# Routing eight images' tokens in groups of one, two, three and two instead of four pairs, with the gate's top two by two maxima

## The chip, the cores and the metric

The kernel runs on one core of one Trainium2 chip. A core has five engines that run side by side, each on its own list of instructions: TensorE (PE; PEld is its loading of weights), VectorE (DVE), ScalarE (ACT), GpSimd (POOL) and SyncE (SP), which here issues the plain DMAs. They wait for each other by semaphores. The metric is the time of one execution on the device in microseconds, from the first to the last instruction with what little lies around it; lower is better.

## What is computed

The input is 8 images of 256 channels and 32 x 32 points, in float32. Two layers follow each other. Cut to what matters:

```python
# layer 0
x = x + vim_block(_ln_c(x))          # a selective scan over the 1024 points, 512 inner channels, 16 states
t = tokens(x)                        # 8 x 1024 tokens of 256
t = t + moe(_ln_t(t))
# moe: 8 experts, each 256 -> 512 -> 256 with gelu; every token takes its two best
probs = softmax(xf @ gate_w + gate_b)
top2_vals, top2_idx = top_k(probs, 2)          # ties: the lower index first
cw = zeros.at[arange(N)[:, None], top2_idx].add(top2_vals)
out = sum over e of cw[:, e] * (gelu(xf @ W1[e] + b1[e]) @ W2[e] + b2[e])
# layer 1
x = x + concat(x_id, conv3x3(x_hw), conv1x11(x_w), conv11x1(x_h), mamba(x_mb))(_ln_c(x))
t = t + mixture_of_depths(_ln_t(t))  # the 511 of 1024 tokens of an image with the largest weights
                                     # pass 256 -> 1024 -> 256, the others stay
```

The routing is independent for each token, so tokens may be gathered and sent to the experts in groups of any size.

## The kernel before

**Units, groups and pairs.** A unit is half an image (512 points). For each of the 16 units layer 0 prepares (`unit_prep`: norm, projections, short convolution, dt) and scans (`scan_unit`): four chunks of 128 channels by 16 states, each with an exponential on ScalarE (L826), a scan on VectorE (L829), a product with C (L834), and the sum over states as matmuls into PSUM (L845). The products with B come from GpSimd (L821), where some pairs of states are added too (L838; how many of the eight pairs of a unit is in `PAIRED`, one entry a unit and four more for the second layer). Rows of B and C come by DMA (`bc`, L880). `tokens` then projects back, writes the tokens to DRAM (`gx`) and makes the gate's logits.

A group is a pair of images, four units, 16 blocks of 128 tokens (NB = 16). When its last unit is done, these follow:

- `route` (L968 to L1101), on VectorE with little else: a softmax over 8 logits; `better` (L999), in eight parts, which compares every logit with every other (128 elements an instruction) and counts how many beat it; `masks` for the first and the second; `counts`, `sums`, `ends`, `ends2`, which give every choice a row in a list sorted by expert and padded to blocks of 256 rows; `pick`, the row's number and the weight for each of the two choices; and the weights turned for the experts' biases (`cwt`).
- `scatter`: each token's normed row is written twice into that list (`slots_x`, DRAM) by indirect DMAs from GpSimd's queue (L1113), 32 for a group.
- `experts`: a group of NB blocks has at most 2 x NB x 128 / 256 + 7 blocks of 256 rows, 23 here. Each reads its rows, one expert's weights (1 MB), turns the rows (L1187), and does two products (L1202 and L1224, gelu on ScalarE between, L1208). Its result leaves PSUM at L1252 and goes to `slots_y`. A block may not start before all row writes of its group have landed.
- `combine`: each token's two result rows come back by indirect DMAs (L1300), are weighted and added, for pairs 0 and 1 by matmuls (L1312 to L1315), for pairs 2 and 3 on VectorE; then layer 1 begins for the same pair: norm, the four convolution branches (`taps_of`, L1391), `mamba_in`, `mamba_scan` (the lines of the unit's scan again), `mamba_out`, `assemble`.
- `ranks` (comparisons of every token's weight with all others, L1601 and L1606), `feed_forward` (row writes, then four blocks of two halves on L1202 and L1224) and `finish`.

**What sets the order.** The whole program is a list of steps, each with an engine, an estimated duration, a priority and the buffers it reads and fills. A planner (`Flow.run`, in Python, before the launch) hands the steps to the engines one by one: of those whose inputs will be ready and whose buffers are free it takes the smallest priority, with some leave to fill gaps. Each engine then runs its steps in that written order, and SP its DMAs. Priorities are positions on one scale: unit i's scan stands at UNIT_AT[i] = 16 + 32 i and takes 32 positions, so the last ends at 544. `PLAN` holds for each pair the positions of its later stages, as (start, step) where there are several parts: `experts=(180, 8.0)` puts block b at 180 + 8 b. Where the planner sees PE idle for over 0.7 us it puts fillers, small matmuls of zeros (L560, L564).

**Buffers.** `logits` has two buffers of [128, 16, 8], `slots_x` two and `slots_y` two lists of 23 x 256 rows in DRAM, `xg` two tiles (a third and fourth once the units are done), `xz` one. The lists `slots_x` are cleared once at the start (`clear_slots`).

Of the kernel before, what the change touches and what calls it, by code (L numbers as in the profile page):

```python
# [47 lines left out]
NB = 16  # L48
NI = NB // 2
SB = 256  # L50

NX = 2 * NB * P // SB + E - 1
# [4 lines left out]
PAIRED = [4, 1, 0, 3, 0, 4, 7, 4, 4, 6, 8, 8, 5, 5, 5, 6, 8, 8, 6, 1]  # L57
# [5 lines left out]
    dict(put=3.51, experts=(180, 8.0), combine=(398, 2.34), taps=(451, 3.28), mamba=464, assemble=(496, 1.12), ranks=500, ffn=(524, 4.8), finish=(613, 2.76)),  # L63
    dict(put=4.68, experts=(357, 6.25), combine=(505, 1.88), taps=(585, 1.2), mamba=551, assemble=(563, 2.41), ranks=620, ffn=(745, 3.84), finish=(768, 4.5)),
    dict(put=5.28, experts=(465, 5), combine=(562, 2.94), taps=(679, 2.65), mamba=643, assemble=(689, 1.5), ranks=682, ffn=(788, 1.69), finish=(797, 4.62)),
    dict(put=2.65, experts=(603, 4), combine=(692, 0.33), taps=(755, 1.54), mamba=775, assemble=(776, 0.43), ranks=753, ffn=(812, 2.4), finish=(841, 3.07)),
# [254 lines left out]
def layers(g, ctx, x, a, out):  # L321
# [71 lines left out]
    first = g.t(w, [P, E, E], "first")  # L393
    nc.gpsimd.memset(first, 0.0)
    for e in range(1, E):
        nc.gpsimd.memset(first[:, e, :e], 1.0)

# [15 lines left out]

    carry = g.t(w, [P, E, NB], "carry")
    nc.gpsimd.memset(carry, 1.0)
    nc.gpsimd.memset(carry[:, :, 0:1], 0.0)

# [36 lines left out]
    groups = [{} for _ in range(B // 2)]  # L454
# [18 lines left out]
    def x_tile(i):  # L473
# [31 lines left out]
        "logits": tiles("logits", [P, NB, E], 2),  # L505
# [5 lines left out]
        "cwt": tiles("cwt", [P, P], 2),  # L511
        "xg": tiles("xg", [P, 2, C], 2, in_order=False),
        "slots_y": tiles("slots_y", [NX * SB, C], 2, where=g.dram),
# [393 lines left out]
    def tokens(i, prio):  # L907

        u = units[i]
        grp, q = groups[i // 4], i % 4  # L910
# [57 lines left out]
    def route(n, prio):  # L968

        grp = groups[n]  # L970
        wide = [P, NB, E]
        r, lg = buf("sq"), grp["logits"]
# [9 lines left out]

        def softmax():
            one = small([P, NB, 1], 0)
            nc.vector.tensor_reduce(one, lg.v, AX.X, ALU.max)
            nc.vector.tensor_tensor(lg.v, lg.v, one.to_broadcast(wide), ALU.subtract)

        def softmax2():
            tot = small([P, NB, 1], 0)
            nc.vector.tensor_reduce(tot, lg.v, AX.X, ALU.add)  # L990
            nc.vector.reciprocal(tot, tot)
            nc.vector.tensor_tensor(lg.v, lg.v, tot.to_broadcast(wide), ALU.mult)


        part_of = [P, NB // 8, E, E]

        def better(part):
            blks = slice(part * NB // 8, (part + 1) * NB // 8)
            gt, eq = small(part_of, 128), small(part_of, 256)  # L999
            mine = lg.v[:, blks].unsqueeze(3).to_broadcast(part_of)  # L1000
            other = lg.v[:, blks].unsqueeze(2).to_broadcast(part_of)
            nc.vector.tensor_tensor(gt, other, mine, ALU.is_gt)
            nc.vector.tensor_tensor(eq, other, mine, ALU.is_equal)
            nc.vector.tensor_tensor(eq, eq, first.unsqueeze(1).to_broadcast(part_of), ALU.mult)
            nc.vector.tensor_tensor(gt, gt, eq, ALU.add)
            nc.vector.tensor_reduce(small(wide, 0)[:, blks], gt, AX.X, ALU.add)

        def sels():
            return [small(wide, 384 + 128 * i) for i in range(3)]

        def masks():
            rank = small(wide, 0)
            sel, sel1, sel2 = sels()
            nc.vector.tensor_scalar(sel, rank, 1.5, None, ALU.is_lt)
            nc.vector.tensor_scalar(sel1, rank, 0.5, None, ALU.is_lt)
# [891 lines left out]
```

## Time and profile before

| | |
|---|---|
| time, median of 3 runs | 3679.84 us (3678.03 to 3680.75) |
| the profiled execution: its time / its span | 3683.03 / 3681.0 us |
| mean granted TensorE clock | 0.946 |
| instructions | 37,497 |
| moved by DMA | 676.61 MB, mean 184 GB/s |

Read by stage: up to about 800 us only units run; from then on the expert blocks of the first groups run beside the scans; pair 0's second layer begins near 1730 us; the last unit's scan ends near 2805 us; then come the last group's routing, its blocks, and the rest of the second layer for pairs 1, 2 and 3. An engine's busy share says little alone: matmuls overlap, so a busy PE isn't PE at its peak, and an engine may be idle where another holds it up.

### The profile page before, as it was taken

The page shows a single profiled execution, that of the slowest core. Times are in us where ns is not written, and L with a number is a line of the kernel's source. Part 1 is how long each engine was busy: PE and PEld are TensorE (multiplying, and loading weights), DVE is VectorE, ACT ScalarE, POOL GpSimd, SP SyncE. Part 2 cuts the span into 40 slices and gives each one's busy share as a digit, 9 for nine tenths or more (in the row PEclk, how much of TensorE's full clock was granted, in tenths as well). Part 3 has the DMA queues.
Part 4 walks back from the last instruction along what each step waited for, and adds up shares of the span by engine and source line. Part 5 has one row for each costly group of instructions (what it writes and reads, how often), then busy time and mean ns, then how long its engine had stood idle before and what let it go on. Part 6 is the DMA issues. An engine that isn't in the chain of part 4 may idle for free. (4 is left out here: it accounts for less than half of the span.)

```text
span 3681.0 us, 37497 instructions
## 1 busy us (share of the span) xinstructions
PE 3211.1 (87%) x10567; PEld 1807.2 (49%) x10567; DVE 2918.0 (79%) x4181; ACT 2188.2 (59%) x3985; POOL 2407.4 (65%) x1751
## 2 busy tenths in 40 slices
PE   8889888889889988978998898988888888899858
PEld 3334333334445444444554445555546565685536
DVE  4889889989778987986988789768698938965951
ACT  4555455467567656755875675655675546747533
POOL 3767567487867758986986887654786743716522
PEclk9999999999999999999999999999999988999989
DMA  6334333346445445644654557565657786877756
GB/s 231 132 132 138 110 125 129 107 161 209 159 133 172 167 134 174 203 155 147 211 178 164 179 178 240 190 197 161 195 180 261 234 258 206 307 230 244 265 168 190
DMA packets 276301, 676.61 MB, mean 184 GB/s; under 512 B 31015, under 2 KB 114861, under 8 KB 276094
## 3 DMA queue, kind: packets, MB, share of 16 engines
q1 hardware_dynamic: 257662, 623.87, 51.6%
q0 software_dynamic: 18432, 50.36, 4.2%
q8 instruction: 84, 1.38, 0.2%
q14 instruction: 123, 1.01, 0.1%
HBM read 572.92 MB, written 101.19 MB: 183 GB/s over the span
## 5 line engine op out<-in xcount | busy, mean ns | idle before, releaser
L821 POOL TENSOR_TENSOR dbu<-dtx,bc 128x1024 f32<-128x1024 f32 x551 | 1300.8, 2374 | 239.7 <-PE y L845 119.6
L845 PE MATMUL y<-dbu,ident 128*128 128x512 f32 x1616 | 837.4, 630 | 174.9 <-POOL dbu L838 129.5
L826 ACT ACTIVATE mm<-dt,neg_a 128x512 f32<-128x512 f32 x1152 | 767.7, 688 | 172.9 <-DVE dbu L834 150.6
L829 DVE TENSOR_TENSOR_SCAN mm<-mm,dbu 128x512 f32<-128x512 f32 x566 | 691.9, 1222 | 211.3 <-ACT mm L826 176.7
L834 DVE TENSOR_TENSOR dbu<-mm,bc 128x512 f32<-128x512 f32 x1104 | 763.3, 691 | 53.1 <-PE mm L1202 0.5
L829 DVE TENSOR_TENSOR_SCAN mm<-mm,state,dbu 128x512 f32<-128x512 f32 x560 | 717.6, 1281 | 40.0 <-ACT mm L826 25.4
L838 POOL TENSOR_TENSOR dbu<-dbu 128x512 f32<-128x512 f32 x318 | 412.0, 1296 | 294.6 <-DVE dbu L834 277.6
L845 PEld LDWEIGHTS y<-dbu,ident 128*128 128x128 f32 x1616 | 291.5, 195 | 537.8 <-issue 211.9
L833 ACT COPY state<-mm 128x1 f32<-128x1 f32 x576 | 91.8, 160 | 701.3 <-DVE dbu L834 660.6
L1224 PE MATMUL mm<-we,hid 128*128 128x256 f32 x1536 | 370.6, 394 | 34.3 <-ACT hid L1208 23.2
L1202 PE MATMUL mm<-xbt,we 128*128 128x256 f32 x1632 | 384.1, 386 | 17.9 <-ACT xbt L1190 10.3
L1202 PEld LDWEIGHTS mm<-xbt,we 128*128 128x128 f32 x1632 | 312.0, 193 | 106.1 <-issue 30.9
L1224 PEld LDWEIGHTS mm<-we,hid 128*128 128x128 f32 x1536 | 296.6, 197 | 116.0 <-ACT hid L1208 35.5
L756 PE MATMUL mm<-pre,w_tap 128*128 128x512 f32 (+3 forms) x512 | 245.2, 622 | 28.8 <-ACT pre L743 27.7
L1300 POOL DMA_INDIRECT ys<-slots_y,slot x128 | 126.9, 992 | 184.8 <-DMA xb<-slots_t 71.3
L560 PE MATMUL y<-still 128*128 128x512 bf16 x924 | 237.5, 392 | 0.0
L462 ACT ACT_TABLE_LOAD x166 | 213.0, 1283 | 3.0
L1208 ACT ACTIVATE hid<-mm,we 128x256 f32<-128x256 f32 x408 | 161.5, 475 | 33.9 <-PE mm L1202 25.1
L756 PEld LDWEIGHTS mm<-pre,w_tap 128*128 128x128 f32 x512 | 97.3, 197 | 167.2 <-issue 106.1
L1688 POOL DMA_INDIRECT ys<-y,slot_t x64 | 64.2, 1003 | 172.8 <-DVE xc L1698 81.0
L560 PEld LDWEIGHTS <-still 128*128 128x128 bf16 x924 | 92.6, 101 | 159.5 <-issue 93.0
L1113 POOL DMA_INDIRECT slots_x<-xg,slot x120 | 122.4, 1020 | 30.8 <-issue 19.7
(279 smaller groups left out, 4476.7 us busy)
## 6 DMA issues: line engine op xcount, KB each, us to landing
bc<-rows SPq DMA_DIRECT2D x610, 512.0 KB
we<-in_W SPq DMA_DIRECT2D x82, 514.0 KB
we<-in_W SPq DMA_DIRECT2D x77, 512.0 KB
xb<-slots_x SPq DMA_DIRECT2D x92, 256.0 KB
slots_y<-xo SPq DMA_DIRECT2D x92, 256.0 KB
xc<-x SPq DMA_DIRECT2D x64, 256.0 KB
we<-in_W12f SPq DMA_DIRECT2D x20, 514.0 KB
slots_x<-xg SPq DMA_DIRECT2D x10, 1024.0 KB
```

The costliest lines, as they stand in the source:

```text
L462: nc.scalar.preload_act_table_set(tables[name])
L560: nc.tensor.matmul(live[0].v[:, 0], still, wide, start=False, stop=False)
L756: nc.tensor.matmul(tc_.v[:, cut:], w_tap[:, c, j], pre.v[:, cut + j : j + N], start=j == 3, stop=j == 0)
L821: gpsimd(2.45, prio, lambda: nc.gpsimd.tensor_tensor(dbu.v, dtxs.v[:, n : n + 1].to_broadcast(wide2), bt.v, ALU.mult), [dtxs, bt], [dbu], ...
L826: step(ACT, 0.69, prio, lambda j=j, h=h: nc.scalar.activation(h.v, dts.v[:, n], AF.Exp, scale=scales(j)), [dts], [h], table="exp", scan=True)
L829: step(DVE, 1.25, prio, lambda j=j, h=h: nc.vector.tensor_tensor_scan(h.v, h.v, dbu.v[:, j], 0.0 if initial is None else initial[1](j), AL ...
L834: step(DVE, 0.68, prio, lambda j=j, h=h: nc.vector.tensor_tensor(dbu.v[:, j], h.v, ct.v[:, j], ALU.mult), [h, ct], [dbu], scan=True)
L838: gpsimd(1.3, prio + 2.3, lambda: nc.gpsimd.tensor_tensor(dbu.v[:, 0], dbu.v[:, 0], dbu.v[:, 1], ALU.add), [], [dbu])
L845: nc.tensor.matmul(y.v[:, n], g.ident, dbu.v[:, j], start=False, stop=stop and (paired or j == 1))
L1202: nc.tensor.matmul(tv[:, f], we[0].v[:, at : at + P], xbt.v[:, k], start=k == 0, stop=k == KC - 1)
L1208: nc.scalar.activation(hid.v[:, f], tv[:, f % 2], func, bias=we[0].v[:, at : at + 1])
L1224: nc.tensor.matmul(to, hid.v[:, f, h * P : (h + 1) * P], we[1].v[:, f * C : (f + 1) * C], start=extra is None and f == 0, stop=f == FC - 1,)
```

## The change

Five things are changed together.

1. **Groups.** `GROUPS = [1, 2, 3, 2]`: image 0 alone, images 1 and 2, images 3 to 5, images 6 and 7. A group is routed when its last image's units are done. Groups have 8, 16, 24 and 16 blocks of tokens and `blocks_of(nb)` = 15, 23, 31 and 23 blocks of rows. Tiles are sized for the largest (NB = 24).
2. **Pairs stay for layer 1.** `combine` and all that follows still goes by pairs of images; pair 0 takes results of groups 0 and 1, pair 1 of groups 1 and 2, pairs 2 and 3 of one group each. The load that opens a combination waits for the results of both groups.
3. **Gate by two maxima.** Instead of the comparisons and the masks, `choose` takes the maximum, marks where it is equal, weights the marks by 8 - e (`turn_of`) and takes their maximum, so that one is left, the lowest index; then the same with 2 taken off the chosen one.
4. **Buffers.** `logits` has one buffer instead of two, `slots_y` three instead of two, `cwt` room for a second turned part (the group of three has 192 columns); `xz` is gone and its tile is taken from `xg`; `first` and `carry` are gone, the latter is filled anew in each `sums`.
5. **Places.** `PLAN` and `PAIRED` have new numbers.

```diff
-NB = 16
-NI = NB // 2
+NI = 8
+GROUPS = [1, 2, 3, 2]
+NB = NI * max(GROUPS)
...
+def blocks_of(nb):
+    return 2 * nb * P // SB + E - 1
+NX = blocks_of(NB)
...
-PAIRED = [4, 1, 0, 3, 0, 4, 7, 4, 4, 6, 8, 8, 5, 5, 5, 6, 8, 8, 6, 1]
+PAIRED = [4, 1, 0, 3, 0, 4, 7, 4, 5, 7, 8, 8, 5, 3, 5, 6, 8, 5, 6, 0]
...
-    dict(put=3.51, experts=(180, 8.0), combine=(398, 2.34), taps=(451, 3.28), mamba=464, assemble=(496, 1.12), ranks=500, ffn=(524, 4.8), finish=(613, 2.76)),
-    dict(put=4.68, experts=(357, 6.25), combine=(505, 1.88), taps=(585, 1.2), mamba=551, assemble=(563, 2.41), ranks=620, ffn=(745, 3.84), finish=(768, 4.5)),
-    dict(put=5.28, experts=(465, 5), combine=(562, 2.94), taps=(679, 2.65), mamba=643, assemble=(689, 1.5), ranks=682, ffn=(788, 1.69), finish=(797, 4.62)),
-    dict(put=2.65, experts=(603, 4), combine=(692, 0.33), taps=(755, 1.54), mamba=775, assemble=(776, 0.43), ranks=753, ffn=(812, 2.4), finish=(841, 3.07)),
+    dict(put=1.76, experts=(110, 12.0), combine=(368, 2.34), taps=(474, 4.1), mamba=464, assemble=(501, 1.41), ranks=482, ffn=(514, 4.8), finish=(608, 2.76)),
+    dict(put=4.68, experts=(249, 7.0), combine=(535, 1.9), taps=(590, 0.72), mamba=595, assemble=(595, 2.0), ranks=668, ffn=(750, 3.84), finish=(776, 4.5)),
+    dict(put=5.28, experts=(411, 4.0), combine=(545, 2.9), taps=(679, 2.65), mamba=643, assemble=(679, 1.5), ranks=690, ffn=(808, 1.69), finish=(794, 4.62)),
+    dict(put=2.65, experts=(597, 4.0), combine=(612, 0.32), taps=(765, 1.54), mamba=715, assemble=(726, 0.69), ranks=753, ffn=(812, 2.4), finish=(853, 3.07)),
...
+    turn_of = g.t(w, [P, 1, E], "turn_of")
+    nc.vector.tensor_scalar(turn_of[:, 0], count[:, :E], -1.0, float(E), ALU.mult, ALU.add)
...
-        "logits": tiles("logits", [P, NB, E], 2),
+        "logits": tiles("logits", [P, NB, E], 1),
...
-        "cwt": tiles("cwt", [P, P], 2),
+        "cwt": tiles("cwt", [P, -(-NB // 16), P], 2),
...
-        "slots_y": tiles("slots_y", [NX * SB, C], 2, where=g.dram),
+        "slots_y": tiles("slots_y", [NX * SB, C], 3, where=g.dram),
...
-        def better(part):
-            blks = slice(part * NB // 8, (part + 1) * NB // 8)
-            gt, eq = small(part_of, 128), small(part_of, 256)
-            mine = lg.v[:, blks].unsqueeze(3).to_broadcast(part_of)
-            other = lg.v[:, blks].unsqueeze(2).to_broadcast(part_of)
-            nc.vector.tensor_tensor(gt, other, mine, ALU.is_gt)
-            nc.vector.tensor_tensor(eq, other, mine, ALU.is_equal)
-            nc.vector.tensor_tensor(eq, eq, first.unsqueeze(1).to_broadcast(part_of), ALU.mult)
-            nc.vector.tensor_tensor(gt, gt, eq, ALU.add)
-            nc.vector.tensor_reduce(small(wide, 0)[:, blks], gt, AX.X, ALU.add)
...
+        def choose(i):
+            left, one, same = small(wide, each), small([P, nb, 1], 5 * each), small(wide, 0)
+            sel, sel1, sel2 = sels()
+            if i:
+                nc.vector.scalar_tensor_tensor(left, sel1, -2.0, lgv(), ALU.mult, ALU.add)
+            val, to = (left, sel2) if i else (lgv(), sel1)
+            nc.vector.tensor_reduce(one, val, AX.X, ALU.max)
+            nc.vector.tensor_tensor(same, val, one.to_broadcast(wide), ALU.is_equal)
+            nc.vector.tensor_tensor(same, same, turn_of.to_broadcast(wide), ALU.mult)
+            nc.vector.tensor_reduce(one, same, AX.X, ALU.max)
+            nc.vector.tensor_tensor(to, same, one.to_broadcast(wide), ALU.is_equal)
+            if i:
+                nc.vector.tensor_tensor(sel, sel1, sel2, ALU.add)
...
+            carry = small([P, E, nb], 2 * each)
+            nc.vector.memset(carry, 1.0)
+            nc.vector.memset(carry[:, :, 0:1], 0.0)
...
-        for part in range(8):
-            step(DVE, 1.9, prio + 1 + 0.25 * part, lambda part=part: better(part), [lg], [r])
-        step(DVE, 0.6, prio + 3, masks, [], [r])
+        for i in range(2):
+            step(DVE, 1.4 + 0.5 * i, prio + 1 + i, lambda i=i: choose(i), [lg], [r])
...
-        for b in range(NX):
+        for b in range(blocks_of(grp["nb"])):
...
-        "xz": tiles("xz", [P, 2, 2 * P], 1),
...
+        both = [groups[group_of[2 * n + i]]["y"] for i in range(2)]
...
-                xc.v, grp["gx"].v[:, at : at + 2]), [grp["gx"], grp["y"]], [xc], claims=[at_a, at_b]).opens = line
+                xc.v, moe["gx"].v[:, at : at + 2]), [moe["gx"], *both], [xc], claims=[at_a, at_b]).opens = line
...
+            if i == 0:
+                xz = buf("xg")
...
-        if i % 4 == 3:
-            n = i // 4
+        b = i // 2
+        n = group_of[b]
+        if i % 2 and b == groups[n]["last"]:
             at = PLAN[n]
             route(n, end + 12)
             scatter(n, end + 16, at["put"])
             experts(n, *at["experts"])
-            combine(n, *at["combine"])
...
+            for n in range(groups[n]["first"] // 2, (b + 1) // 2):
+                at = PLAN[n]
+                combine(n, *at["combine"])
...
+                finish(n, *at["finish"])
```

## The prediction

> **What bounds the kernel now.** I read the page first (shares per engine), then the busy time by stage, then the groups of instructions by line, the waits, and last the stretch after the last scan in order of time. The stages are cut where the work changes: no expert block before 800 us, scans beside blocks to 2800, routing of the last group to 2980, its blocks to 3290, the last pair's second layer to 3535, and a closing chain. Columns: stretch, its length, busy us (instructions) of PE, PEld, DVE, ACT and POOL, granted clock, DMA share, GB/s.
>
> ```profile
> span 3681.0 us, 37497 instructions
> PE 3211.1 (87%) x10567; PEld 1807.2 (49%) x10567; DVE 2918.0 (79%) x4181; ACT 2188.2 (59%) x3985; POOL 2407.4 (65%) x1751
> ...
> 0.00:800.00 800.00, 693.52 (x1793) 295.44 (x1793) 665.64 (x836) 416.40 (x764) 500.56 (x331) 0.94 0.41 139
> 800.00:2000.00 1200.00, 1065.71 (x3352) 575.10 (x3352) 1007.70 (x1257) 781.11 (x1390) 941.62 (x643) 0.97 0.52 171
> 2000.00:2800.00 800.00, 706.48 (x2315) 409.21 (x2314) 663.70 (x886) 521.13 (x938) 563.13 (x396) 0.94 0.60 192
> 2800.00:2980.00 180.00, 149.40 (x628) 111.16 (x627) 134.69 (x196) 98.80 (x182) 102.74 (x103) 0.95 0.72 238
> 2980.00:3290.00 310.00, 273.21 (x1164) 201.20 (x1163) 226.87 (x537) 185.92 (x351) 133.44 (x115) 0.93 0.79 259
> 3290.00:3535.00 245.00, 223.67 (x890) 145.26 (x891) 182.68 (x355) 137.22 (x265) 122.03 (x110) 0.96 0.70 233
> 3535.00:3681.00 146.00, 99.07 (x432) 69.79 (x430) 36.71 (x118) 47.59 (x98) 43.92 (x55) 0.84 0.58 180
> ```
>
> To 2800 us VectorE is busy 83 to 84% of every stage and the others wait for it. The longest wait of all is ScalarE's for VectorE's product with C (L834). After 2800 TensorE is the fullest, at 83 to 91%, and at the very end nobody is: one chain runs.
>
> ```profile
> ACT state L833 <- DVE dbu L834: 660.6, 467, 8.0
> POOL dbu L838 <- DVE dbu L834: 277.6, 161, 10.0
> ```
>
> The gate is VectorE work. Its five instructions, 32 of each (eight parts in each of four groups): name, shapes, count, busy us, mean ns, idle before.
>
> ```profile
> L1002 DVE TENSOR_TENSOR sq<-logits 128x128 f32<-128x128 f32 x32 | 21.9, 683 | 0.7
> L1004 DVE TENSOR_TENSOR sq<-sq,first 128x128 f32<-128x128 f32 x32 | 19.5, 610 | 1.1
> L1003 DVE TENSOR_TENSOR sq<-logits 128x128 f32<-128x128 f32 x32 | 18.8, 587 | 0.0
> L1005 DVE TENSOR_TENSOR sq<-sq 128x128 f32<-128x128 f32 x32 | 12.5, 389 | 1.1
> L1006 DVE TENSOR_REDUCE sq<-sq 128x16 f32<-128x128 f32 x32 | 9.2, 286 | 1.1
> ```
>
> The last group's way from gate to experts, in order of time: the gate's first and last instruction on VectorE, the last of 32 row writes on POOL, the first block's transposes on PE (start, length).
>
> ```profile
> 2825.89 0.29 DVE L985 TENSOR_REDUCE sq<-logits 128x16 f32<-128x128 f32 x1 [1.48 <-POOL logits L962]
> 2899.17 0.28 DVE L1083 TENSOR_TENSOR sq<-sq,logits 128x128 f32<-128x128 f32 x1
> 2955.81 0.96 POOL L1113 DMA_INDIRECT slots_x<-xg,slot  x1 [0.19 <-issue]
> 2983.29 0.60 PE L1187 MATMUL mm<-ident,xb 128*128 128x128 f32 x4
> ```
>
> So 157 us pass, 73 of them in a gate whose own instructions fill some 38; the other 35 are pair 1's scans (L829) and taps (L1391).
>
> **The change, part by part.** The sum is made against the profiled execution, 3683.03 us (span 3681.0 and 2.0 around it), which is 3.2 above the median of 3679.84.
>
> *Gate.* Removed: 81.9 us of comparisons (the five rows) and the masks, four times three instructions of 226, 218 and 530 ns, 3.9 us. Added per group: 4 reductions (286 ns, the L1006 row) and 8 with two inputs (567 ns, the mean of the first four rows), 5.7 us; two small fills and one more sum, 0.9. Four groups: 26.4. Net -59 us of VectorE, 14.8 a group. Uncontended, at the medians of 292 ns of the same rows, 46.6 would go and 18 come: -30 with masks. If the new ones hardly wait and the old waits vanish, -69. I take 59: these are means over the places where the gate runs. [...] The trace's means decide.
>
> Three of the four gates lie before 2800, where VectorE is busy 0.85 of the time (2290 of 2700 us from 100 us on); what it saves there turns into time by about that share: 3 x 14.8 x 0.85 = **-38** (bounds 0 and -52). If VectorE were hidden there, the cover would be ScalarE's exponentials (688 ns each), and the term is 0.
>
> *Blocks.* Their number is unchanged: a group of n images has 8n + 7, so 15 + 23 + 31 + 23 = 92 against four times 23. PE's expert work stays. What moves is when they can run: the first 15 from position 110 instead of 23 from 180. Block evictions (L1252) by stage are now 0, 32, 30, 7 and 23 or 24; so 7 blocks of the first three groups run after 2800. At the tail's own pace (transposes 8.3 us apart between 3215 and 3256) these are 58 us of PE. Started some 250 us earlier, at the 2.7 blocks per 100 us of the stage from 800 on, 7 blocks are in front by 800 us, so the backlog goes. Against that pair 1's combination, now at 2553 to 2669, must wait for group 2 and falls near or behind 2800: 128 matmuls at 0.22 us (16 take 3.62) are 28 us. Net -30, times PE's share of 0.88 from 2980 to 3290: **-26**. Bounds: 0 (PE not the limit) and -58. [...]
>
> *Cost of an early block on the scans.* A block uses no VectorE; VectorE idles 11.5% from 100 to 800 without blocks and 16% from 800 to 2000 with 2.7 per 100 us, about 1.3 to 1.7 us a block, paid now wherever the block stands: **0**. If the earlier, denser scans suffer more: +20 (15 blocks), bound below -10.
>
> *Last gate.* Its own 15 us go, and pair 1's scans and taps move from positions 551 and 585 to 595 and 590, behind the gate at 556: up to 50 of its 73 us. Its row writes (32, one per 1.27 us, at least 41 us of the 53) now share POOL's queue with gathers of two combinations instead of one, placed at 535 and 545: 32 gathers at 1.0 us, of which I let 24 fall into it. **-26**, bounds -60 and +20. The blocks behind it wait for all the writes, and PE has little else then.
>
> *The tail's order.* Pair 3's combination 692 to 612, scan 775 to 715, assembly 776 to 726, its feed-forward unmoved at 812, its end 841 to 853; pair 2's feed-forward 788 to 808. PE does only fillers and closing transposes for 50 us from 3536, so a feed-forward left over for there would gain up to 50; queues crossed badly on SP or POOL lose as much. **0**, bounds -50 and +50. In the same way pairs 0's places (combination 398 to 368, taps 451 to 474, ranks 500 to 482) are 0 within ±15.
>
> *Small ones, together 0 within -10 and +25.* Clearing 31 instead of 23 blocks of two buffers is 16 transfers of 1 MB for 12, 4.2 MB, 18 us of DMA at the first 100 us' 231 GB/s, on SP's queue among the row loads for which POOL already waits 74 us before 800; the DMA share of 0.41 there hides it. The combination's turned tile now takes one of xg's buffers and can hold up a row write. The combination's load waits for both groups' results; behind it in SP's order stand later loads, whose users are later too. The paired additions stay 70 for the units and fall from 23 to 19 for the second layer: 8 fewer on POOL at 1.3 us, 16 more matmul instructions at 0.63. A second transpose and eviction in the group of three: 0.3 and 0.4.
>
> Sum: -38 - 26 - 26 = -90; 3683 - 90 = 3593, and 3590 against the median.
>
> **The rivals.**
> 1. *Pair 1 is pushed too far (slower).* Its combination needs the 31 blocks of group 2. From 2000 to 2800 blocks came at 3.75 per 100 us; 31 of them from about 2050 end near 2880, not at 2553. Then taps (26 at 1.6 us), scans (32 at 1.95) and assembly of pair 1, some 117 us of VectorE, fall into 2980 to 3535, where VectorE has 145 us idle in all. If they don't fit between the dependences, the price is 117, with the gates' 53 gained and nothing else: 3683 + 64 - 3 = 3744. It decides once more than 90 us don't fit. For it: stages already at 73% of VectorE and 90% of PE. Against: 2800 to 2980 is freed, and the blocks start earlier.
> 2. *The order of the tail gains too.* All 50 us of empty PE near the end are filled: 3540. For it: the gap is in the trace. Against: ranks, row writes and feed-forward of pair 3 are one chain.
> 3. *The gate was cover.* If ScalarE or POOL takes the place of VectorE in the scans (POOL 78%, ACT 65% from 800 to 2000), only a third of the scans' term remains and half the blocks': 3683 - 13 - 13 - 3 = 3654. Against: the 660 us of ScalarE's waiting for VectorE.
> 4. *Nothing moves*, gains and losses equal: 3680.
>
> **How the numbers follow.** What I count as seen is 0.2%, 7 us, about what a measurement of this kernel can tell from no change. My forecast 0.42, with its own range 3560 to 3625; rival 2 0.20; rival 3 0.15, nearly all of it faster; rival 1 0.18; rival 4 0.05. Faster 0.42 + 0.20 + 0.14 = 0.76, same 0.06, slower 0.18. The range holds eight in ten: down to 3525 leaves out a third of rival 2, up to 3710 the greater part of rival 1.
>
> **What would show it.** Right: VectorE's total near 2860 us; the first block's eviction before 600 us; no block of the first three groups after the last unit's scans (now about 2805), and these ending 40 to 50 us earlier; the last gate in under 45 us and 130 us or less from it to the first block. Wrong: pair 1's scans in the middle of the last group's blocks with those at 14 us apiece or more; VectorE's share to 2800 falling while ScalarE's or POOL's waits grow; more than 90 us from the last group's last block to pair 3's scan.

## The result, and the profile after

The changed kernel takes 3708.74 us (median of 7 runs, 3695.41 to 3719.39) against 3679.84 us (7 runs, 3674.72 to 3687.13). The ratio is 1.007 with a 95% interval of 1.0053 to 1.0088: slower by 0.7%, some 26 to 29 us, where 90 us less were forecast. Its profiled execution took 3698.3 us, at the quick end of its runs, 15.3 more than that of before; so the stages below account for 15 of the 29.

The page after, span and totals, and its busy time by the stretches used before (length; PE, PEld, DVE, ACT, POOL; granted clock; DMA share; GB/s; the first stretch is left out):

```profile
span 3696.6 us, 37546 instructions
...
PE 3228.2 (87%) x10632; PEld 1820.2 (49%) x10632; DVE 2866.2 (78%) x4070; ACT 2191.4 (59%) x3988; POOL 2375.0 (64%) x1744
```

```profile
800.00:2000.00 1200.00, 1059.77 (x3306) 570.20 (x3305) 989.92 (x1194) 767.19 (x1354) 925.98 (x614) 0.96 0.50 164
2000.00:2800.00 800.00, 696.45 (x2362) 411.44 (x2361) 633.17 (x841) 512.01 (x913) 535.65 (x395) 0.94 0.60 196
2800.00:2980.00 180.00, 158.23 (x568) 96.89 (x566) 96.38 (x170) 90.26 (x186) 113.79 (x141) 0.89 0.60 196
2980.00:3290.00 310.00, 273.38 (x1124) 193.49 (x1123) 248.72 (x474) 187.55 (x357) 147.63 (x120) 0.96 0.79 262
3290.00:3535.00 245.00, 218.20 (x854) 142.07 (x854) 197.71 (x423) 140.73 (x271) 120.04 (x110) 0.94 0.75 248
```

VectorE does 51.8 us less, and most of the gap is simply idle: in 2000 to 2800 it was busy 663.7 us and is busy 633.2. The two longest waits for it, which were 660.6 and 277.6 us:

```profile
ACT state L838 <- DVE dbu L839: 626.9, 445, 12.8
POOL dbu L843 <- DVE dbu L839: 315.2, 148, 15.0
```

ScalarE waits 34 us less and GpSimd 38 us more: the time that VectorE no longer works is not time that the scans no longer take. Where the time went is seen in the order of time (start, length): first and last of the 48 row writes of the group of three (L1135), the end of unit 13 (the last matmul of `tokens`, L938), the group's first and last result (L1274), the end of unit 15, then the last group's first and last gate instruction, its last row write and the transposes of its first block.

```profile
2030.32 1.05 POOL L1135 DMA_INDIRECT slots_x<-xg,slot  x1 [0.68 <-ACT xg L1174]
2274.03 0.40 PE L938 MATMUL mm<-res,x 128*128 128x136 f32 x2
2311.01 0.97 POOL L1135 DMA_INDIRECT slots_x<-xg,slot  x1 [0.19 <-issue]
2345.42 0.57 ACT L1274 COPY xo<-mm 128x512 f32<-128x512 f32 x1
2758.63 0.58 ACT L1274 COPY xo<-mm 128x512 f32<-128x512 f32 x1 [0.50 <-PE mm L1246]
2855.86 0.39 PE L938 MATMUL mm<-res,x 128*128 128x136 f32 x2
2859.68 0.29 DVE L998 TENSOR_REDUCE sq<-logits 128x16 f32<-128x128 f32 x1 [2.26 <-POOL logits L968]
2876.61 0.29 DVE L1096 TENSOR_TENSOR sq<-sq,logits 128x128 f32<-128x128 f32 x1
2929.61 0.97 POOL L1135 DMA_INDIRECT slots_x<-xg,slot  x1 [0.19 <-issue]
2950.06 1.09 PE L1209 MATMUL mm<-ident,xb 128*128 128x128 f32 x4 [7.29 <-DMA xb<-slots_x]
```

The same moments of both profiled executions, in us (a unit's end is its last matmul of `tokens`, a block's moment is its result leaving PSUM):

| | before | after | difference |
|---|---|---|---|
| unit 3 / 7 / 11 ends | 646 / 1272 / 1926 | 671 / 1313 / 1920 | +25 / +41 / -6 |
| unit 13 ends | 2277 | 2274 | -3 |
| third group's blocks | 23, 2397 to 2980 | 31, 2345 to 2759 | |
| unit 14 / 15 ends | 2652 / 2821 | 2695 / 2856 | +43 / +35 |
| last gate | 73 long | 17 long | |
| last group's first / last block | 2990 / 3279 | 2973 / 3290 | -17 / +11 |
| pair 1's `mamba_out` begins | 2937 | 3079 | +142 |
| span | 3681 | 3697 | +16 |

The early groups cost 41 us by unit 7 and give them back by unit 11. The last result of group 1 leaves at 1920, the first of the group of three at 2345: 425 us without a block. Then 31 come in 414 us, and unit 14 pays for them. The short last gate wins half of it back, and the last group's blocks, now with pair 1's scans between them, take 317 instead of 289 us.

The hole and the crowd, by busy time from unit 11's end to 13's and from 13's to 14's, before and after:

```profile
1926.00:2277.00 351.00, 309.29 (x1008) 175.46 (x1007) 305.64 (x388) 224.83 (x418) 272.21 (x208) 0.96 0.58 187
2277.00:2652.00 375.00, 329.69 (x1095) 195.52 (x1094) 293.74 (x474) 231.70 (x453) 223.71 (x154) 0.93 0.59 188
```

```profile
1920.00:2274.00 354.00, 288.52 (x765) 129.17 (x764) 290.32 (x366) 191.39 (x380) 283.45 (x234) 0.87 0.47 153
2274.00:2695.00 421.00, 375.58 (x1406) 247.77 (x1405) 304.96 (x455) 276.63 (x493) 218.60 (x148) 0.97 0.63 205
```

With 1 block instead of 12 the first stretch is as long as before; with 26 instead of 15 the second is 46 us longer.

### The profile page after: what moved, and what is told of

It is laid out like the page before. It is cut to its first block, busy times and chain, and to the rows that moved or that the text cites. A ratio compares the mean times of both kernels' runs of the same rounds, so it can differ in the third digit from the quotient of the medians.

```text
span 3696.6 us, 37546 instructions
## 1 busy us (share of the span) xinstructions
PE 3228.2 (87%) x10632; PEld 1820.2 (49%) x10632; DVE 2866.2 (78%) x4070; ACT 2191.4 (59%) x3988; POOL 2375.0 (64%) x1744
## 2 busy tenths in 40 slices
DMA packets 278669, 680.81 MB, mean 184 GB/s; under 512 B 31079, under 2 KB 115437, under 8 KB 278462
## 5 line engine op out<-in xcount | busy, mean ns | idle before, releaser
L850 PE MATMUL y<-dbu,ident 128*128 128x512 f32 x1650 | 846.6, 628 | 169.5 <-POOL dbu L843 124.6
L834 DVE TENSOR_TENSOR_SCAN mm<-mm,state,dbu 128x512 f32<-128x512 f32 x570 | 730.6, 1282 | 45.0 <-POOL dbu L826 25.1
L843 POOL TENSOR_TENSOR dbu<-dbu 128x512 f32<-128x512 f32 x311 | 398.4, 1281 | 322.8 <-DVE dbu L839 315.2
L850 PEld LDWEIGHTS y<-dbu,ident 128*128 128x128 f32 x1650 | 302.2, 197 | 544.3 <-issue 246.4
L1246 PE MATMUL mm<-we,hid 128*128 128x256 f32 x1616 | 385.6, 391 | 30.9 <-ACT hid L1230 23.2
L1246 PEld LDWEIGHTS mm<-we,hid 128*128 128x128 f32 x1616 | 309.1, 195 | 117.7 <-ACT hid L1230 41.9
L565 PE MATMUL y<-still 128*128 128x512 bf16 x983 | 256.8, 397 | 0.0
L804 POOL TENSOR_TENSOR dt<-dt,sq 128x1024 f32<-128x1024 f32 x34 | 80.7, 2374 | 128.6 <-ACT sq L798 79.4
```

The lines of the kernel that those rows point to most:

```text
L565: nc.tensor.matmul(live[0].v[:, 0], still, wide, start=False, stop=False)
L834: step(DVE, 1.25, prio, lambda j=j, h=h: nc.vector.tensor_tensor_scan(h.v, h.v, dbu.v[:, j], 0.0 if initial is None else initial[1](j), AL ...
L843: gpsimd(1.3, prio + 2.3, lambda: nc.gpsimd.tensor_tensor(dbu.v[:, 0], dbu.v[:, 0], dbu.v[:, 1], ALU.add), [], [dbu])
L850: nc.tensor.matmul(y.v[:, n], g.ident, dbu.v[:, j], start=False, stop=stop and (paired or j == 1))
L1246: nc.tensor.matmul(to, hid.v[:, f, h * P : (h + 1) * P], we[1].v[:, f * C : (f + 1) * C], start=extra is None and f == 0, stop=f == FC - 1,)
```

## The experiments

My first theory was that of the forecast, VectorE's time in the scans turns into time, with the loss lying in the groups' places; the rivals were that the gate's time is cover, and that late rows or the crowd of blocks make the loss. All ratios are against runs of the kernel before on the same chip. Moments and stretches in us are read from one profiled execution each and set beside the one of before (3683 us). On the chips of the experiments before took 3668 to 3677 us in the median, and up to unit 3's end, ahead of every gate, kernels in the very same order already lie up to 5 us apart (646, 644 and 641 in before and experiments 5 and 6); a difference of a few us in such a moment shows nothing.

**1. Four pairs with the new gate.** The changed kernel with pairs and the places of before.

```diff
-GROUPS = [1, 2, 3, 2]
+GROUPS = [2, 2, 2, 2]
-PAIRED, PLAN: the changed kernel's
+PAIRED, PLAN: those of before
```

> The changed kernel with GROUPS = [2, 2, 2, 2] and the PLAN and PAIRED of before: gate by two maxima and the new buffers, without the groups and the places. Theory (the groups lose what the gate wins: no expert block runs from 1921 to 2345 us, then 31 crowd beside units 14 and 15): faster than before by the gate's share, 20 to 45 us, so 3635 to 3660. Rival G (VectorE's time in the gate was cover, and the gate saves nothing): within 8 us of before, 3672 to 3688. Rival B (the turned tile taken from xg, or the single logits buffer, cost time): slower than before, 3690 or more.

Measured: 3678.21 us, ratio 1.0006 [0.9993, 1.0019]. VectorE's total fell from 2918.0 to 2870.4 us, the time not at all: the theory's saving did not come. Gate and buffers together change nothing, so groups and their places carry the loss.

**2. The changed kernel with the old gate.**

```diff
-            step(DVE, 1.4 + 0.5 * i, prio + 1 + i, lambda i=i: choose(i), [lg], [r])
+        for part in range(nb // 2):
+            step(DVE, 1.9, prio + 1 + 2.0 * part / (nb // 2), lambda part=part: better(part), [lg], [r])
+        step(DVE, 0.6, prio + 3, masks, [], [r])
```

> The changed kernel with the old gate (comparisons, two blocks of tokens an instruction, and masks). Theory: the gate is worth about as much here as with pairs, so 20 to 45 us slower than the changed kernel, 3725 to 3755. Rival G: within 10 us of the changed kernel, 3695 to 3720.

Measured: 3725.57 us, ratio 1.0123 [1.0104, 1.0142], 0.53% or some 20 us above the changed kernel. With the groups the new gate is worth that, although the order is written anew here too, and without it the change would have lost 45 us.

**3. Rows of the group of three written sooner.**

```diff
-    dict(put=5.28, experts=(411, 4.0), ...
+    dict(put=3.52, experts=(411, 4.0), ...
```

> The changed kernel with the row writes of the group of three placed every 3.52 positions instead of 5.28, so that its 12 steps span the 42 positions that 8 steps of 5.28 span before. Theory: its first block comes near 2200 us instead of 2345, the blocks crowd less, unit 14 gets back 15 to 40 us: 3665 to 3695. Rival P (not the late rows but the layer-1 work of pair 1 in the tail is what costs): first block earlier, time within 10 us of the changed kernel, 3698 to 3718. Rival Q (the denser writes hold up the scans' products on POOL): slower than the changed kernel by 15 or more.

Measured: 3751.58 us, ratio 1.0195 [1.0173, 1.0218]. The last row is written at 2243 instead of 2311 and the first block leaves at 2279 instead of 2345, but unit 13 ends at 2358 instead of 2274 and unit 15 at 2889 instead of 2856. The stretch from unit 11's end to 13's now has 8 blocks, the one to unit 14's end 20:

```profile
1925.00:2358.00 433.00, 347.67 (x1041) 179.14 (x1041) 362.90 (x413) 237.68 (x458) 320.88 (x257) 0.88 0.52 170
2358.00:2715.00 357.00, 322.50 (x1156) 204.76 (x1157) 232.87 (x399) 218.91 (x399) 162.35 (x99) 0.97 0.56 179
```

The hole is narrower and the kernel slower by 46 us: lateness of the rows alone is not the cause. Rival Q named the sign (slower by 15 or more); that the denser writes hold up GpSimd's products, its reason, is not shown.

**4. The groups in the places of before.**

```diff
-PAIRED, PLAN: the changed kernel's
+PAIRED, PLAN: those of before
```

> The changed kernel's groups and gate with the PLAN and PAIRED of before, which were made for pairs. Theory: group 0 starts at 180 as before, group 2's 31 blocks stand at 465 to 615 and so reach 70 positions behind the last scan; pair 1 waits for them. 100 us or more slower than the changed kernel, 3810 or more. Rival P' (places matter little beside the groups themselves): within 40 us of the changed kernel.

Measured: 3964.86 us, ratio 1.0775 [1.0747, 1.0802]. The places belong to the groups; the changed kernel's numbers save most of the 285 us that uneven groups cost in the places made for pairs.

**5. The new gate in an unchanged order.** The kernel before; `choose` runs in two of the eight comparison steps, the others are empty, and all keep their declared length, so that the planner writes the old order.

```diff
+            if part in (0, 4):
+                choose(part // 4)
-            (the comparisons)
```

> The kernel before with the new gate alone: its two choices stand where the first and the fifth of the eight comparison steps stood, the other six steps are empty, and every step keeps its declared length, so that the written order of all other work is that of before, pairs and places too. VectorE should lose about 47 us in all (2918 to about 2870). Theory V (VectorE's time in the scans turns into time by its share, the gate term of the prediction): the end comes 25 to 50 us earlier, ratio 0.986 to 0.993. Rival C (the scans go by the chain from engine to engine and the written order, VectorE has slack there): units 7, 11 and 15 end within 8 us of before (968, 1926, 2821), and at most the last gate's own some 15 us appear, ratio 0.995 to 1.001.

Measured: 3651.52 us, ratio 0.9949 [0.9933, 0.9965]. Unit 11 ends at 1910 (1926), unit 15 at 2805 (2821). The page's totals:

```profile
PE 3194.9 (88%) x10567; PEld 1803.1 (49%) x10567; DVE 2870.0 (79%) x4058; ACT 2189.7 (60%) x3985; POOL 2403.3 (66%) x1743
```

48 us less of VectorE are worth 0.51%, 18.7 us, four tenths. That is under theory V's 25 and, at 0.9949, on the edge of rival C, which allowed some 15 us for the last gate's own way. The profiles show both parts. From unit 15's end to the last group's first block 154 us pass instead of 169. From unit 3's end, ahead of the first gate, to unit 15's it is 2161 instead of 2175, where rival C had the scans take the time up again. (Unit 7 ends at 1263 against 1272; the 968 in the expectation is unit 5's end.) How the 18.7 us split between the two is not shown: this profile lies 38 us under that of before, twice as much, so half of the difference is chip and execution.

**6. The old gate twice, in the same order.**

```diff
+            for _ in range(2):
+                compare(part)
```

> The kernel before with every comparison of its gate done twice, same declared lengths, hence the same written order: some 82 us more of VectorE, 20 a group. Theory V: three gates in the scans cost 3 x 20 x 0.85 = 51 us and the last one up to 20, ratio 1.013 to 1.019. Rival C: each gate only holds up the work right behind it; the scans take most of it up again, ratio at most 1.006, and units 7 and 11 end within 8 us of before.

Measured: 3730.18 us, ratio 1.0166 [1.0145, 1.0186], in theory V's range, but by luck: its sum took 82 us more of VectorE, and busy time rose by 45 us only (2918.0 to 2963.0). By theory V's own sum these would give some 40 us; the time rose by 61, more than one for one. Here added work costs what removed work does not give back; why, these runs do not settle.

**7 and 8. What ate the 0.5%: the order or the buffers?** Seven: buffers and places of before, the new gate declared at its own short length. Eight: the changed kernel's buffers, the gate declared as long as before.

```diff
 (7: on the kernel of 5)
-        for part in range(8):
-            step(DVE, 1.9, prio + 1 + 0.25 * part, ...
-        step(DVE, 0.6, prio + 3, masks, [], [r])
+        for i in range(2):
+            step(DVE, 1.4 + 0.5 * i, prio + 1 + i, ...
 (8: on the kernel of 1, the same lines the other way round)
```

> Four pairs, the places and the buffers of before, with the new gate declared at its own two short steps (1.4 and 1.9 instead of eight of 1.9), so that the work around it is written in a new order. With the same gate in the old order the kernel was faster by 0.5% (0.9949); with the new gate, new order and the changed kernel's buffers it was not (1.0006). Theory O (the order that is written around a shorter gate gives the gain away): 0.998 to 1.002. Rival S (the buffers give it away: one logits tile instead of two, the combination's tile taken from xg): 0.993 to 0.997 here.

> Four pairs and the places of before, with all the changed kernel's buffers and its gate, the gate declared as long as before. Theory O: the buffers cost nothing, 0.993 to 0.997. Rival S: they cost some 15 to 20 us, 0.998 to 1.003. If both this and the kernel with the old buffers lie at 0.998 or above, either change of the written order is enough to lose it.

Measured: 3679.0 us, 1.0008 [0.9999, 1.0016], and 3673.1 us, 0.9991 [0.998, 1.0003]. Both lose it. In both, unit 15 still ends earlier than before (2813 and 2804 against 2821). What they lack against the unchanged order lies behind it: from there to the end they need 858 and 870 us, like before (860), and the unchanged order 838. So the gate may speed up the scans a little here too (from unit 3's end to 15's 2168 and 2161 us against 2175, within what chip and execution can do), and either way of writing the order anew loses what it is worth at the end. Two things are left open: the unchanged order ran on another chip than these two, each against before there, and in eight new order and new buffers come together.

**9. A hole, with pairs.** The kernel before; it leaves out the products and the gelu of the second pair's blocks, which only pass their rows on.

```diff
+            if n == 1:
+                to_slots(xb, grp["y"], b, now + 1.5)
+                continue
```

> The kernel before, but the 23 expert blocks of the second pair (beside units 10 to 13) are not computed: their rows are loaded and written on as they are. 32 + 32 + 4 matmuls a block are gone, by the rows of before some 25 us of TensorE a block, 23 x 25 = 280 us at these durations and less where they overlap. Theory H (a block beside the scans is nearly free while there are at most some 16 to a unit, so a hole without blocks gains nothing): units 11 and 13 end within 25 us of before (1926, 2277), the end is at most 40 us earlier, ratio 0.988 to 1.0. Rival B (each block has a fixed price of 4 us or more wherever it stands, so a hole is paid back): unit 13 ends 90 us or more earlier, ratio below 0.977.

Measured: 3617.6 us, ratio 0.9858 [0.9838, 0.9879], 52 us for 23 blocks, between the two. By place theory H is right: unit 11 ends at 1910 (1926) and unit 13 at 2266 (2277), with 2 blocks left between them instead of 12. Not all of the hole is free: it begins at 1707, and from unit 9's end to 11's, with 3 blocks instead of 10, 316 us pass instead of 330. Most of the gain comes after: the third pair's blocks start at 2231 instead of 2397, 8 instead of 15 stand before unit 14's end, and that stretch falls from 375 to 338 us. From unit 11's end to 13's and 13's to 14's:

```profile
1910.00:2266.00 356.00, 278.21 (x751) 128.40 (x749) 317.55 (x390) 183.92 (x348) 276.59 (x205) 0.87 0.45 151
2266.00:2604.00 338.00, 285.87 (x908) 153.38 (x908) 291.88 (x471) 197.60 (x396) 216.70 (x144) 0.94 0.53 173
```

**10. A smaller crowd.** The changed kernel; it leaves out the products and the gelu of 8 of the group of three's 31 blocks, which only pass their rows on.

```diff
+            if n == 2 and b % 4 == 3 or n == 2 and b == 30:
+                to_slots(xb, grp["y"], b, now + 1.5)
+                continue
```

> The changed kernel, but 8 of the 31 expert blocks of the group of three are not computed, every fourth and the last: their rows are loaded and written on as they are. So 23 remain, as many as a pair has. Theory H (31 blocks beside two units are a crowd, and each above some 16 to a unit costs about 4 to 5 us): unit 14 gets back most of its 46 us more, unit 15 ends about 2821 instead of 2856, the end is 25 to 45 us earlier than the changed kernel's, ratio to before 0.995 to 1.002. Rival L (the loss comes from the rows being late and not from the number of blocks): at most 10 us, ratio 1.004 to 1.009.

Measured: 3679.51 us, ratio 1.0029 [1.0015, 1.0042], some 15 us below the changed kernel. The stretch to unit 14's end, now with 20 computed blocks:

```profile
2283.00:2675.00 392.00, 341.28 (x1215) 212.27 (x1214) 297.00 (x452) 250.01 (x446) 203.12 (x128) 0.95 0.62 201
```

Unit 15 ends 26 us earlier (2830). In this profiled execution, the slowest of its ten (3698 us), all of that is lost behind it (866 us to the end instead of 840); by the ratios some 15 us are left. With experiments 9 and 10 the stretch has four points: 338 us with 8 blocks, 375 with 15, 392 with 20, 421 with 26. That is (421 - 338) / 18 = 4.6 us a block, though other work in it differs too (28 gathers with pairs, none with the groups), while the stretch ahead has 356, 351 and 354 us with 2, 12 and 1 blocks. Theory H is right on the place; the 25 to 45 us at the end were too many. At the end the crowd's blocks are worth no more than others: 15 us for 8 here, 1.9 apiece, and 52 us for 23 in experiment 9, 2.3 apiece. Experiment 3 bounds it too: with its order the stretch ahead took 433 us with 8 blocks and this one 357 with 20, so the price belongs to a place in a written order and is no constant of a block.

**11. Pair 1's scans behind the last gate, with pairs.** The kernel of experiment 5 with the changed kernel's places for that.

```diff
-taps=(585, 1.2), mamba=551, assemble=(563, 2.41)
+taps=(590, 0.72), mamba=595, assemble=(595, 2.0)
```

> The kernel with the new gate in the old order (0.9949), with one step moved: taps, scans and assembly of pair 1 go from 585, 551 and 563 to the changed kernel's 590, 595 and 595, behind the last group's gate. Term 'last gate' of the prediction: the gate falls from some 67 to under 30 us and the end comes up to 26 us earlier, ratio 0.987 to 0.993. Rival 1 of the prediction (the scans then stand in the last group's blocks and cost more there than they free): the blocks take 13 us or more apiece instead of 12.4, and the end is 10 to 60 us later than with the scans in front, ratio 0.998 to 1.012.

Measured: 3704.01 us, ratio 1.0069 [1.0055, 1.0084], against 0.9949 without the move: 44 us lost. The last group's blocks, first to last, without the move and with it:

```profile
2959.00:3245.00 286.00, 251.81 (x1078) 185.72 (x1076) 211.78 (x471) 176.77 (x331) 127.91 (x109) 0.95 0.80 263
```

```profile
2936.00:3276.00 340.00, 295.65 (x1216) 198.99 (x1215) 250.92 (x492) 198.99 (x378) 168.49 (x136) 0.95 0.76 255
```

The gate falls from 67 to 29 us and the first block leaves 23 us earlier, as the term had it; the 23 blocks then take 54 us more (39 us of VectorE and 44 us of PE, fillers included, have come between them; 14.8 instead of 12.4 us a block), and the stages behind lose another 33. Together that is 64 us in the profiled executions, the slowest here and the quickest there; by the ratios it is 44.

**12, 13 and 14. Each grouping in places of its own.** Open was whether the numbers or the groups lose. The planner's written list has an end of its own, in its estimated durations; `PLAN` and `PAIRED` were varied at random and kept when that end came earlier, for four pairs, for the change's groups, and for groups of 2, 2, 3 and 1, all with the changed kernel's gate and buffers.

```diff
 (12: GROUPS = [2, 2, 2, 2])
+    dict(put=3.43, experts=(179, 6.9), combine=(401, 1.84), taps=(486, 3.32), mamba=464, assemble=(500, 0.76), ranks=509, ffn=(524, 3.66), finish=(708, 2.15)),
+    dict(put=6.53, experts=(342, 6.25), combine=(505, 2.17), taps=(650, 1.33), mamba=551, assemble=(582, 1.59), ranks=528, ffn=(705, 6.41), finish=(722, 3.82)),
+    dict(put=6.6, experts=(465, 5), combine=(558, 1.49), taps=(668, 4.35), mamba=633, assemble=(704, 1.01), ranks=665, ffn=(774, 1.37), finish=(827, 3.22)),
+    dict(put=16.61, experts=(586, 3.73), combine=(646, 0.68), taps=(746, 1.48), mamba=741, assemble=(744, 3.71), ranks=742, ffn=(837, 1.84), finish=(1058, 1.41)),
+PAIRED = [5, 4, 0, 4, 1, 5, 5, 8, 4, 6, 8, 7, 6, 5, 8, 8, 3, 8, 6, 0]
 (13: GROUPS = [1, 2, 3, 2]; 14: GROUPS = [2, 2, 3, 1]; other numbers likewise)
```

> Four pairs, the changed kernel's buffers and gate, with new numbers in PLAN and PAIRED: the best of some 1,000 variations by the end of the planner's own written list, 3520 against 3571 with the old numbers. Theory P (the list's end follows the chip to about 1%, as it did for the four kernels run first): 40 to 60 us faster than before, ratio 0.984 to 0.990. Rival W (the planner's gains on paper are within the scatter that a new order brings, some 20 us): 0.993 to 1.004. Beside the next kernel, which had as many variations: what four pairs and four uneven groups are worth, each in places of its own.

> Groups of one, two, three and two, the changed kernel in all but the numbers in PLAN and PAIRED: the best of some 850 variations by the end of the planner's own list, 3594 against 3608 with the changed kernel's numbers. Theory G (the loss belongs to the groups: pair 1's second layer must wait for 31 blocks and so stands in the last group's blocks wherever the rest is put): ratio 1.001 to 1.008, 50 us or more behind the pairs searched alike, pair 1's scans still beside the last group's blocks, at 13 us or more apiece. Rival N (only the numbers were badly chosen): within 15 us of the pairs searched alike.

> Groups of two, two, three and one: pair 1 takes results of group 1 alone and needn't wait for the group of three, and the last group has 15 blocks instead of 23; numbers in PLAN and PAIRED by the same search, 3596 by the planner's list. If waiting for 31 blocks hurts only through pair 1, this should reach the searched pairs within 20 us or beat them, the last blocks being 8 fewer (some 100 us less of blocks at the end). If the group of three hurts whoever follows it (here pair 2, which needs its 31 blocks, whose rows come only after unit 13), it lies with the groups of one, two, three and two: ratio 1.000 to 1.009.

Measured: pairs 3621.97 us, ratio 0.985 [0.9819, 0.9882]; the change's groups 3702.67 us, 1.0072 [1.005, 1.0094]; groups of 2, 2, 3 and 1 3707.72 us, 1.0088 [1.0064, 1.0111]. The stretch from unit 13's end to 14's with pairs, and those from unit 11's to 13's and 13's to 14's with the change's groups:

```profile
2255.00:2588.00 333.00, 298.35 (x988) 173.55 (x987) 287.75 (x424) 213.54 (x421) 225.73 (x153) 0.94 0.59 193
```

```profile
1914.00:2343.00 429.00, 355.63 (x1100) 192.65 (x1101) 365.75 (x417) 251.42 (x481) 317.34 (x252) 0.90 0.55 184
2343.00:2679.00 336.00, 298.17 (x1047) 185.71 (x1045) 237.28 (x404) 216.14 (x392) 157.69 (x100) 0.96 0.56 182
```

The pairs beat both kernels, by 1.5% and, through the two ratios, by 2.2%. The same search leaves the groups where the change has them, 81 us behind; it moves the loss from the stretch to unit 14's end (337 us) into the one ahead (429), and unit 15 still ends at 2841 where the pairs reach 2777. Theory G is right on the time; the last blocks took 12.8 us apiece and not 13 or more. With 2, 2, 3 and 1 pair 1 need not wait for the group of three, and 8 blocks fewer stand at the end; yet the 31 blocks run from 2569 to 3066, and unit 15 ends at 2855. So the loss comes with the group of three in both groupings, whichever pair follows it, in the best places that this search found. What exactly its 31 late blocks displace stays open: the stretch that grows is not the same in the three kernels with such a group (to unit 14's end 421 us with 26 blocks in the changed kernel and 428 with 11 with 2, 2, 3 and 1; to unit 13's end 429 with 11 in the searched one), only the sum at unit 15 is (2856, 2841, 2855).

## Why the prediction was wrong, point by point

- **The failing steps** are *Blocks* together with *Cost of an early block on the scans*, together some 45 us at unit 15 (35 later than before, where the three re-ordered kernels with pairs and the new gate have it 8 to 17 earlier), and the share of 0.85 in *Gate*. By place: -90 was forecast and +15 measured in the profile, a gap of 105; the scans were to end 40 to 50 us earlier and ended 35 later, which is 75 to 85 of it. That the groups carry the loss is shown (experiments 1 and 12 to 14); by what mechanism the late blocks hold up the scans is shown only in part (experiments 3, 9 and 10).
- *Blocks* (-26) counted blocks by stage and let the backlog go. It does go: the first result leaves at 521 us, and the last of the first three groups at 2759, before unit 15 ends. But the step did not ask when the rows of the group of three would be there. Group 1 runs dry at 1920, the 48 row writes last from 2030 to 2312, and 31 blocks remain for the 510 us to unit 15's end. The step *Cost of an early block* (0, up to +20) held that a block costs the scans about the same wherever it stands. In the changed kernel nothing was gained from the hole and 46 us were lost in the crowd; taking 8 blocks out of the crowd gave 29 of them back there. At the end it gave some 15, no more apiece than a block of a pair (experiment 9), so that a block costs more in the crowd is shown for that stretch alone.
- *Gate*. -59 us of VectorE were forecast; the total fell by 51.8, and the four routes from some 138 to 85 us. That count was nearly right. The prediction's other count, at the medians of 292 ns, made it 30: in the last gate, beside which GpSimd ran no large product, the two-input instructions of 128 elements did take 0.29 to 0.32 us, while in the first gate two of 64 elements took 1.46 and 2.27. But turning 14.8 us a gate into time by VectorE's busy share was wrong: 48 us in all four gates gave 18.7 in the unchanged order, 15 of them perhaps on the last gate's own way, and nothing in three orders written anew with pairs (with the groups some 20, experiment 2). Rival 3, *the gate was cover*, is right that far: of the 38 us for the scans 14 show in the old order at unit 15's end, about a third, and in those three orders the end gives the gain away.
- *Last gate* (-26) was right in size by luck. From unit 15's end to the last block it is 458 us before and 434 after, -24. But the way to the first block fell by 52 (gate 73 to 17 us, gate to first transposes 157 to 90), and 28 are lost again in the blocks, for which the term had nothing. The 24 us that it set against the gain, gathers among the row writes, did not come: no gather of a combination stands there, and from the gate's end to the last row write it is 54 us, 57 before. With pairs the same move loses 44 us, so its sign hangs on what stands behind.
- *The tail's order* (0): from the last block to the end 402 and 407 us; pair 3's scan still begins 125 us behind the last block, 128 before, so the sign of being wrong at 90 us was there from the start and told nothing. *Small ones* (0): 4.2 MB more by DMA, as counted (676.61 to 680.81 MB); unit 3 ends 25 us later and unit 7 41, given back by unit 11.
- Rival 1, *pair 1 is pushed too far*, had the right sign and mechanism: its `mamba_out` begins 142 us later, between the last blocks, which take 317 / 23 = 13.8 us each. Its price of 117 us was too high, 28 there, and its blocks came otherwise: 31 blocks at the pace of the stage would have ended at 2880, but they came twice as fast, at the scans' expense, and ended at 2759.
- All signs of being right came but one (VectorE 2866 us, first result 521, backlog gone, gate 17, 90 to the first block). The one that did not, scans ending 40 to 50 us earlier, is the one that tests how the gains turn into time.
- The sign *VectorE's share to 2800 falling while ScalarE's or POOL's waits grow* did show: 83 to 79% in the stage from 2000, GpSimd's wait from 278 to 315 us.

## What to carry to other kernels

Count work not only by stage but by when its inputs are there: here 31 blocks that came late all at once cost the scans beside them some us apiece, and the emptiest stretch ahead of them gave nothing back. Where a planner writes the order, a saved microsecond is tested twice, once in the unchanged order for its own worth and once in the new one; here the new order alone moved the time by some 0.5% (0.9949 and 1.0008, on two chips). And where the planner computes the end of its own list, read it before changing its places: 3577 before, 3608 with the change, 3520 and 3594 for the searched pairs and groups and 3596 for 2, 2, 3 and 1, that is +31, -57, +17 and +19, stand beside +26, -55, +26 and +32 us on the chip. It is a hint and no more: run on the kernels of experiments 2 and 11 the planner ends at 3658 and 3638, +81 and +61, and the chip lost 45 and 25.

## What the runs showed of the hardware

A busy VectorE was partly a waiting one here. In the changed kernel's first gate (VectorE and GpSimd, in order of time):

```profile
404.06 4.65 POOL L826 TENSOR_TENSOR dbu<-dtx,bc 128x1024 f32<-128x1024 f32 x2 [4.89 <-DMA bc<-rows]
...
405.04 1.46 DVE L1018 TENSOR_TENSOR sq<-logits,sq 128x64 f32<-128x64 f32 x1
406.53 2.27 DVE L1019 TENSOR_TENSOR sq<-sq,turn_of 128x64 f32<-128x64 f32 x1
408.83 0.22 DVE L1020 TENSOR_REDUCE sq<-sq 128x8 f32<-128x64 f32 x1
409.08 0.22 DVE L1021 TENSOR_TENSOR sq<-sq 128x64 f32<-128x64 f32 x1
```

The two GpSimd products end at 406.41 and 408.71; VectorE's two two-input instructions of 64 elements end at 406.50 and 408.80, after 1.46 and 2.27 us, and the same kind takes 0.22 us once GpSimd is idle. The reductions were not drawn out: all 32 of the old gate took 285 to 289 ns, where the comparison that opens each part (L1002) took 258 to 3164. In the changed kernel's third gate a reduction of 192 elements that began at 1953.46, while a GpSimd product ran (1953.18 to 1955.63), took 0.35 us, like the other three reductions of that gate's two choices, and the two-input instruction behind it 2.00 us, to 1955.85. That VectorE waits there for GpSimd's product to end is read from these ends; what makes it wait is not shown.

The granted TensorE clock was lower in the two stretches with hardly a block: 0.87 with 765 matmuls and 1 block (the changed kernel) and with 751 and 2 (experiment 9) in some 355 us, where the kernel before had 0.96 with 1008 and 12. The count of matmuls alone does not make it: from 350 to 700 us the kernel before has 0.96 with 796. The lower clock may be part of why a hole gives little back; that was not tested by itself.
